# A fused attention and gated feed-forward kernel on one core: the side work of the last token pair placed by hand

## The chip, the core and the metric

The kernel runs on one core of a Trainium2 chip. A core has a matrix engine (TensorE, PE in the profile, with its weight loads as PEld), a vector engine (VectorE, DVE), a scalar engine (ScalarE, ACT), GpSimd (POOL), and a sync engine (SP) that here does little but issue DMA transfers, in the order of its own queue. Every engine runs its instructions in order and waits for others by semaphores. The metric is the device time of one execution in microseconds (us). Times below are medians of several runs; the profile is of one execution.

## The reference

x has two sequences of 2048 tokens with 2048 features, in float32. The output is x plus an attention and a feed-forward part, both of the normalised x:

```python
xn = _layernorm(x)
qkv = xn @ Wqkv + bqkv            # 2048 -> 3 * 512
q, k, v = split(qkv)              # one head, d = 512
attn = softmax(q @ k.T / sqrt(512)) @ v @ Wo + bo

q2 = xn @ Wq_w.T                  # router, 16 wide
top_vals, top_idx = top_k(q2 @ keys.T, 16)       # 16 of 64 experts
gate = one_hot sum of softmax(top_vals)
z = (xn @ A_w.T).reshape(64, 8) * gate           # rank 8 for each expert
ffn = z @ B_w.T * 2.0

out = x + attn + ffn
```

## The kernel before, in words

*Arithmetic.* Every float32 operand of a large matmul is split into a high part (`split_hi`, a cast on ACT, line 121) and a remainder (`split_lo`, a subtraction on DVE, line 124); a `product` (line 129) is three matmuls. Matrices are multiplied by a scheme of seven products in place of eight (P1, P2, P6, P5, P3, P7, P4), so operands and results are sums and differences of quarters.

*Stages.* Tokens go in 8 blocks of 512, two blocks make a pair. First all projections (q, k, the feed-forward z, v) are made: the first pair by itself, then pairs 1 to 3 in `phase`, seven phases for each pair. A phase has seven items: six feature pieces of 24 groups of matmuls with 512 columns, 5.45 us each at full pace, then V, the values and the router, in two pieces of 48 matmuls with 264 columns, 5.8 us each; some 44 us in all. For each piece `fetch` (line 605) issues the load of the weight `pw` on SP and splits it; `pw` has three slots to load into. After each item its results are evacuated (`phase_out`) and put down for a store; the stores are issued at the end of the next item (`flush`, line 162): q to `q_d`, k to `k_d`, values to `v_d`, z to `oz_d`. Then come the scores: `score(g)` (matmuls on line 1081), 56 for each pair of query blocks, each of six matmuls of 512 columns, 1.36 us, in step with the softmax and with the weighting of the values of the pair before. The output stage (line 1355) comes last, from 2029.7 us on.

*Side work.* `beside(j, ph)` gives each phase a list of small steps, and `phase` cuts the list into seven parts, one after each item. They are issued behind that item's instructions in the program; a scheduler then merges them with what is around. For pairs 1 and 2 the side work prepares the next pair's x. The last pair has no next pair, and prepares the scores:
- `key_list(a, b)`: keys 0 to 7 out of 16. A key (256 of the 512 features of a block of 512 tokens) loads two tiles `kr` from `k_d`, and has seven steps, one for each product. A step has at most one sum (lines 851 to 857), a cast and a subtraction into a tile `kst` of 512 words (line 124 and 121), and the store of the step before it to `kp_d` (line 843). The ring of `kst` has four slots, shared with the tiles `ev` and `zt` of the phases' results; in P4 it is a ring of three other slots.
- `query_steps(j, ring)`, pair 0's in P3 and P7, pair 1's in P4: twice, for d = 0 and 1, four loads of `qs` from `q_d` (line 892), four sums (lines 895 to 898), four stores to `qs_d` (line 902). The ring of four slots for pair 1 is `mid(0, 1, 2, 3)`, whose first two are also the slots of the value tiles `vs`.
- `query_load` and `query_split`: seven operands `qt` for a pair, one for each product (load on line 915), from `q_d` or `qs_d`. In P4 of the last pair `query_ready(0, n)` loads operand n + 1 and splits operand n.

The split operands `t` of the next phase are side work too (`split_steps`), and so are the sums in front of them. `mixed` interleaves several lists evenly.

*The first scores.* The operands `kt` of the scores are loaded back from `kp_d` (`key_load(i)`, line 937, two steps in a tile). Four of them are issued before the loop over g, the next after every second score. Side work of the score stages is put down for a g by `deal`: keys 8 to 11 beside the scores of the first pair (g from 0 to 55), keys 12 to 14 beside the second's, key 15 beside the third's, `query_steps` of pairs 2 and 3 and the preparation of the output weights (`combos`) later. NG1 is 56.

SP takes all loads and stores named here in one queue. A DMA on it waits for the landing of the one eight places before it, besides what its own data need.

The lines that matter for the order of P4's side work:

```python
ks["st"] = Ring(sb, "H6", "B18", "B19")
return [], [lambda: query_load(0, 0)] + mixed(
    [lambda n=n: query_ready(0, n) for n in range(7)],
    key_list(7, 8, False) + query_steps(1, mid(0, 1, 2, 3)),
)
```

Of the kernel before, what the change touches and what calls it, by code (L numbers as in the profile page):

```python
# [9 lines left out]
FR = mybir.dt.float32r  # L10
# [6 lines left out]
P = 128  # L17
# [45 lines left out]
def attn_ffn_kernel(ctx: ExitStack, tc, x, xT, wq, wv, wob, bqk, bv, bo, keysT, out):  # L63
# [17 lines left out]
    def big(*js):  # L81
        return Ring(sb, *(f"B{j}" for j in js))
# [569 lines left out]
    def mixed(*lists):  # L652

        n = max(map(len, lists))
        return [
            st for k in range(n) for ls in lists
            for st in ls[k * len(ls) // n : (k + 1) * len(ls) // n]
        ]

    def beside(j, ph):  # L660

        b00, b01, b10, b11 = (0, 0), (0, 1), (1, 0), (1, 1)
        more = j + 1 in PAIRS
        s0, s1 = stat_steps.get(2 * j + 2), stat_steps.get(2 * j + 3)
        if ph == "P1":
            t3 = sum_steps(j, nc.vector, b01, b11, b01, ALU.subtract)
            n10, n01, n11 = x_steps(j, *b10), x_steps(j, *b01), x_steps(j, *b11)
            if j > PAIRS[0]:
                return [], mixed(split_steps(j, "P2", *b10), n01[1], n11[1], t3)
            return (  # L670
                [n10[0], n01[0], n11[0]],
                mixed(n10[1], split_steps(j, "P2", *b10)) + mixed(n01[1], n11[1]),
            )
        if ph == "P2":
            t3 = sum_steps(j, nc.vector, b01, b11, b01, ALU.subtract) if j == PAIRS[0] else []
            return [], mixed(
                t3, sum_steps(j, nc.vector, b00, b01, b00, ALU.add), split_steps(j, "P6", *b00)
            )
        if ph == "P6":
            return [], mixed(  # L680
                sum_steps(j, nc.vector, b10, b10, b00, ALU.subtract),
                sum_steps(j, nc.vector, b00, b11, b00, ALU.subtract), split_steps(j, "P5", *b00),
                s0[:-2] if more else key_list(0, 3),
            )
        if ph == "P5":
            if more:
                steps = mixed(split_steps(j, "P3", *b11), s1[:-2])
                return [], s0[-2:-1] + steps[:6] + s0[-1:] + steps[6:]
            return [], mixed(split_steps(j, "P3", *b11), key_list(3, 5))
        if ph == "P3":  # L690
            if more:
                n = x_steps(j + 1, *b00)
                steps = mixed(split_steps(j, "P7", *b01), n[1][:2])
                return n[0], s1[-2:-1] + steps[:3] + s1[-1:] + steps[3:]
            return [], mixed(
                split_steps(j, "P7", *b01), query_steps(0, big(*GROUPS[3]), (0,))
            )
        if ph == "P7":
            if more:
                n = x_steps(j + 1, *b10)  # L700
                return n[0], mixed(split_steps(j, "P4", *b10), n[1][:2])
            return [], mixed(
                split_steps(j, "P4", *b10), query_steps(0, big(*GROUPS[3]), (1,)), key_list(5, 7)
            )
        if more:
            return x_steps(j + 1, *b01)[0] + x_steps(j + 1, *b11)[0], mixed(
                x_steps(j + 1, *b00)[1][2:], split_steps(j + 1, "P1", *b00)[:2],
            ) + mixed(split_steps(j + 1, "P1", *b00)[2:], x_steps(j + 1, *b10)[1][2:])
        ks["st"] = Ring(sb, "H6", "B18", "B19")
        return [], [lambda: query_load(0, 0)] + mixed(  # L710
            [lambda n=n: query_ready(0, n) for n in range(7)],
            key_list(7, 8, False) + query_steps(1, mid(0, 1, 2, 3)),
        )

    XU, YU, XV, YV = {}, {}, {}, {}

# [49 lines left out]
    def phase(j, ph, n):  # L766

        loads, steps = beside(j, ph)
        if not loads or callable(loads[0]):
            loads = [loads]  # L770
        ops = [tsp[j, ph, cp] for cp in range(NCP)]
        qr, gx = None, {}
        i = 2 * j + (ph in ("P3", "P7"))
        for m, it in enumerate(ITEMS[ph]):
            with behind("sp"):
                for st in loads.pop(0) if loads else []:
                    st()
            ps = [acc() for t in range(NT)] if it == "V" else acc()
            for g in range(2 if it == "V" else 1):
                w = ready.pop(n)  # L780
                n += 1
                if it != "V":
                    for c in range(HC):
                        product(
                            ps, lambda a: w[a][:, c * P : (c + 1) * P],
                            lambda b: ops[c // 2][b][:, c % 2, :], c == 0, c == HC - 1,
                        )
                else:
                    for cc in range(HC // 2):
                        c = g * HC // 2 + cc  # L790
                        for t in range(NT):
                            sl = slice(t * P, (t + 1) * P)
                            product(
                                ps[t][:, :VH], lambda a: ops[c // 2][a][:, c % 2, sl],
                                lambda b: w[b][:, cc, :], c == 0, c == HC - 1,
                            )
                fetch(n + 1)
            flush()
            if it == "V" and ph in ("P2", "P3"):
                qr = router_in()  # L800
            if it == NFP - 2:
                if qr is not None:
                    with behind("pe"):
                        gfs[i] = gates(i, wk)
                h = ph in ("P7", "P4")
                gx = {2 * h + k: gate(gfs[i], 2 * h + k) for k in range(2)} if ph in ("P2", "P3", "P7", "P4") else {}
            phase_out(j, ph, it, ps, qr, gx)
            if qr is not None and it in (0, 1):
                with behind("pe"):
                    if it == 0:  # L810
                        qT = router(qr)
                    else:
                        wk = choose(qT)
            for st in steps[m * len(steps) // 7 : (m + 1) * len(steps) // 7]:
                with behind("sp", "pe", "dve"):
                    st()
        return n
# [4 lines left out]
    ORDER = ("P1", "P6", "P2", "P5", "P3", "P7", "P4")  # L822
    NPAIR = NB // 2
    NKS = NK // 2
    ks = {"R": Ring(sb, "B25", "B26", "H7", "H8"), "st": big(27, 28, 29, 9)}
    qop, kop = {}, {}

    def key_steps(kb, d):


        v = {}
# [13 lines left out]
        def one(step):  # L845
            a00, a01, a10, a11 = (quad(a, h) for a in range(2) for h in range(2))
            tt = nc.vector.tensor_tensor
            out()
            src = {"P1": a00, "P2": a01, "P4": a11, "P5": a11, "P7": a10, "P6": a00, "P3": a01}[step]
            if step == "P5":  # L850
                tt(a11, a10, a11, ALU.add)
            if step == "P7":
                tt(a10, a00, a10, ALU.subtract)
            if step == "P6":
                tt(a00, a11, a00, ALU.subtract)
            if step == "P3":
                tt(a01, a01, a00, ALU.subtract)
            st = ks["st"]([P, 2, 2, P], FR, "kst")
            split_hi(st[:, :, 0, :], src)
            split_lo(st[:, :, 1, :], src, st[:, :, 0, :])  # L860
            v["out"] = kp_d[kb][ORDER.index(step)][:, :, :, d, :], raw(st)
# [56 lines left out]
    def query_split(j, n):  # L918
        hi, lo = qop[j, n]
        split_hi(hi, raw(lo))  # L920
        split_lo(lo, raw(lo), hi)

    def query_ready(j, n):
        if n + 1 < 7:
            query_load(j, n + 1)
        query_split(j, n)

    def key_load(i):

# [74 lines left out]
    n = 0  # L1004
# [23 lines left out]
    r_tp = mid(0, 1, 2, 3)  # L1028
    r_ph = wide(0, 1, 2)
    r_vt = wide(3, 4, 5, 9)  # L1030
    ks = {"R": mid(0, 1, 2, 3), "st": wide(0, 1, 2, 3, 4, 5)}
    S, tag_of, mbc, pt_, M, L, av, rl_, vt_, lsum = {}, {}, {}, {}, {}, {}, {}, {}, {}, {}
    ones = mid(2)([P, P], F32, "ones")
    nc.vector.memset(ones, 1.0)
# [376 lines left out]
    total = NPAIR * NG1  # L1411

    begin = [NG1 * (j + 1) + (9 if j in (0, NPAIR - 1) else 5) for j in range(NPAIR)]
    for i in range(4):
        key_load(i)
    side = {}

    def deal(g, steps, every=1):
# [11 lines left out]
        for k, st in enumerate(steps):  # L1430
            deal(g + (0, 3, 4)[k % 3] + 5 * (k // 3), [st])

    for n in range(4):
        keys(8 + n, 3 + 11 * n, 11 * n - 3 if n else 0)

    def small_ring():
        ks["R"], ks["st"] = mid(0, 1), mid(2, 3)

    deal(NG1 + 2, [small_ring])
    for n, g in ((12, NG1 + 6), (13, NG1 + 18), (14, NG1 + 49), (15, 2 * NG1 + 10)):  # L1440
        keys(n, g, g - 3)
    spaced(NG1 + 36, query_steps(2, r_tp))
    spaced(2 * NG1 + 19, query_steps(3, r_tp))
    slots = [2 * NG1 + k for k in (35, 40, 45)] + [3 * NG1 + k for k in (7, 12, 17, 22, 35)]
    for k, g in enumerate(slots):
        spaced(g, combos(k // ND, k % ND))

# [145 lines left out]
```

## Time and profile before

| | us |
|---|---|
| runs | 2637.84 median of 3 (2637.28 to 2642.51) |
| the profiled execution | 2639.59 |
| its span | 2637.8, at a granted TensorE clock of 0.994 |
| last pair's P6 ends, P5 starts | 1147.6 |
| last pair's P4, first scores | 1283.8 to 1335.4, 1335.4 to 1420 |
| second to fourth score stages, output stage | 1420 to 2029.7, from 2029.7 |

The profile names engines, lines and tiles: `PE L129 MATMUL acc<-t,pw` is a matmul of `product` that reads the tiles t and pw. In a timeline a row has its start, the time that it took, and how many such instructions ran in it one after the other; in brackets stands how long the engine was idle before it, and what released it. A list of waits adds these by line and releaser: total, times, longest. Rows on SP are issues of DMAs; the transfer lands some us later. In the part on DMA issues the last column is the median time from issue to landing.

### The profile page before, as it was taken

To read this page: it belongs to the slowest core of one execution; us is meant where nothing else is said; L and a number is where in the kernel's file an instruction comes from. 1 tells how busy PE (TensorE), PEld (TensorE's weight loads), DVE (VectorE), ACT (ScalarE), POOL (GpSimd) and SP (SyncE) were. 2 spreads that over 40 slices of the span, in tenths; PEclk is the share of its full clock that TensorE was granted. 3 is DMA by queue.
4 is the path that set the end of the run, shared out by engine and by line. 5 is a ranking of instruction groups with operands and counts; after the bars stand their busy time and mean duration, and the time that the engine had idled before them with its cause. 6 is when DMAs were issued, how large, how long until landed. Compare 5 with 4: busy or idle time off the path is not lost. (4 is left out here: it accounts for less than half of the span.)

```text
span 2637.8 us, 34791 instructions
## 1 busy us (share of the span) xinstructions
PE 2600.1 (99%) x12689; PEld 2194.4 (83%) x12689; DVE 1994.4 (76%) x2827; ACT 860.0 (33%) x1249; POOL 523.7 (20%) x315
## 2 busy tenths in 40 slices
PE   8999999999999999999989999999999999999999
PEld 7889888888888888888877887878777888888887
DVE  7557649867878677776769979979698776797675
ACT  4323323323332323343323434333254222332221
POOL 1311420001000010000000000000000666566664
PEclk9999999999999999999999999999999999999999
DMA  6667875668446673576999898889688554565542
GB/s 234 225 249 264 280 274 175 208 221 277 149 137 230 212 269 126 187 235 213 294 335 322 264 336 281 295 312 315 202 279 294 176 170 166 178 220 174 177 164 100
DMA packets 348043, 608.10 MB, mean 231 GB/s; under 512 B 28456, under 2 KB 151392, under 8 KB 347872
## 3 DMA queue, kind: packets, MB, share of 16 engines
q1 hardware_dynamic: 334912, 575.99, 65.1%
q10 hardware_dynamic: 12960, 29.89, 3.4%
q8 instruction: 100, 1.64, 0.3%
q14 instruction: 71, 0.58, 0.1%
HBM read 450.42 MB, written 155.35 MB: 230 GB/s over the span
## 5 line engine op out<-in xcount | busy, mean ns | idle before, releaser
L129 PE MATMUL acc<-t,pw 128*128 128x512 f32 x3024 | 697.4, 391 | 4.3 <-ACT t L121 1.8
L129 PEld LDWEIGHTS acc<-t,pw 128*128 128x128 f32 x3024 | 567.3, 188 | 123.8 <-ACT t L121 2.2
L1355 PE MATMUL acc<-wb,s 128*128 128x512 f32 x2688 | 609.8, 389 | 0.1
L1355 PEld LDWEIGHTS acc<-wb,s 128*128 128x128 f32 x2688 | 504.6, 188 | 105.1 <-ACT u L1367 0.6
L1339 POOL TENSOR_TENSOR xo<-xo,bo_bc 128x512 f32<-128x512 f32 x128 | 212.2, 1665 | 906.5 <-DMA bo_bc<-in_bo 612.8
L129 PE MATMUL acc<-ph,vt 128*128 128x512 f32 x1536 | 378.7, 391 | 4.4 <-issue 1.8
L1081 PE MATMUL acc<-qt,kt 128*128 128x512 f32 x1344 | 338.8, 394 | 9.1 <-DMA kt<-kp_d 5.5
L129 PEld LDWEIGHTS acc<-ph,vt 128*128 128x128 f32 x1536 | 288.7, 188 | 67.6 <-issue 3.2
L1081 PEld LDWEIGHTS acc<-qt,kt 128*128 128x128 f32 x1344 | 254.1, 190 | 67.3 <-DVE sp L1102 5.1
L121 ACT CAST pw<-pw 128x1024 fp32r<-128x1024 f32 (+1 forms) x168 | 177.7, 1059 | 343.2 <-PE acc L129 244.0
L124 DVE TENSOR_TENSOR pw<-pw 128x1024 fp32r<-128x1024 f32 (+1 forms) x168 | 213.0, 1268 | 78.6 <-ACT pw L121 77.9
L129 PE MATMUL acc<-xh,wh 128*128 128x512 f32 x1152 | 263.6, 390 | 0.0
L129 PEld LDWEIGHTS acc<-xh,wh 128*128 128x128 f32 x1152 | 215.6, 188 | 44.9
L129 PE MATMUL acc<-pw,t 128*128 128x264 f32 x2016 | 248.4, 285 | 4.6 <-ACT pw L121 3.7
L129 PEld LDWEIGHTS acc<-pw,t 128*128 128x128 f32 x2016 | 247.4, 189 | 6.3 <-ACT pw L121 3.9
L121 ACT CAST s<-xz 128x1024 fp32r<-128x1024 f32 x112 | 118.0, 1054 | 367.7 <-PE acc L1355 302.1
L124 DVE TENSOR_TENSOR s<-xz,s 128x1024 fp32r<-128x1024 f32 x112 | 172.8, 1545 | 39.4 <-ACT s L121 39.2
L124 DVE TENSOR_TENSOR wh<-wu,wh 128x512 fp32r<-128x512 f32 x96 | 84.1, 893 | 95.8 <-ACT wh L121 93.7
L518 POOL TENSOR_TENSOR zt<-zt,g 128x512 f32<-128x512 f32 x24 | 40.1, 1683 | 507.1 <-DMA g<-gd 241.4
L1344 DVE TENSOR_TENSOR xo<-xo,acc 128x512 f32<-128x512 f32 x128 | 86.9, 680 | 52.0 <-POOL xo L1385 25.3
L124 DVE TENSOR_TENSOR t<-xq,t 128x1024 fp32r<-128x1024 f32 x84 | 107.5, 1283 | 18.6 <-ACT t L121 18.1
L121 ACT CAST t<-xq 128x1024 fp32r<-128x1024 f32 x84 | 88.3, 1051 | 92.9 <-DVE xq L648 38.2
(165 smaller groups left out, 2508.3 us busy)
## 6 DMA issues: line engine op xcount, KB each, us to landing
vt<-v_d SPq DMA_DIRECT2D x128, 512.0 KB, 5.2
kt<-kp_d SPq DMA_DIRECT2D x224, 256.0 KB, 5.2
pw<-sq_d SPq DMA_DIRECT2D x72, 512.0 KB, 4.1
xo<-in_x SPq DMA_DIRECT2D x128, 256.0 KB, 3.1
xz<-oz_d SPq DMA_DIRECT2D x64, 512.0 KB, 4.6
out_y<-xo SPq DMA_DIRECT2D x128, 256.0 KB, 2.5
kp_d<-kst SPq DMA_DIRECT2D x112, 256.0 KB, 4.5
pw<-in_wq SPq DMA_DIRECT2D x54, 512.0 KB, 4.5
```

What stands on the lines that cost most here:

```text
L121: return nc.scalar.copy(hi, src)
L124: return (eng or nc.vector).tensor_tensor(lo, src, raw(hi), ALU.subtract)
L129: last["pe"] = nc.tensor.matmul(ps, st(a_), mv(b_), start=first and n == 0, stop=end and n == 2)
L518: nc.gpsimd.tensor_tensor(zt, zt, gx[n], ALU.mult)
L1081: last["pe"] = nc.tensor.matmul(ps, k[:, a, d, :], q[c][:, d, :], start=not more and d == 0 and i == 0, stop=d == 1 and i == 2, skip_group ...
L1339: nc.gpsimd.tensor_tensor(xs, xs, bo_bc[q // (NB // 2 * NH), c], ALU.add)
L1344: nc.vector.tensor_tensor(xs, xs, ps, op)
L1355: nc.tensor.matmul(ps, st[a_][:, kk, sl], mv[b_], start=not more and kk == 0 and n == 0, stop=kk == ND - 1 and n == 2, skip_group_check=more,)
```

## The change

1. `ks["n"]` is new: with 2, two steps of a key share one `kst` slot of 1024 words, the second step in the second half; seven steps take four slots in place of seven. With `small_ring` (from g = 58 on) it is 1, as before.
2. In P6, P5 and P7 of the last pair the last five, four and four key steps are no longer interleaved with the other side work, but come after it, at the end of the phase.
3. P4 of the last pair gets its side work by item, as a list of seven lists. `query_ready` goes; queries are loaded one step further ahead of their splits. The second group of query steps (load `l0`, `l1`, sums `s0`, `s1`, stores `o0`, `o1`) begins with the first item, where it stood at the end. The first four `key_load` move from in front of the loop over g into the last two items. The `kst` ring is `big(18, 19)`, two slots for two steps each.
4. Beside the first scores go three keys (8 to 10, at g = 5 + 14n, with their loads at 14n) in place of four. Key 11 takes the second stage's first place, the later keys are shifted by one place, and loads come two places ahead, not three.
5. `query_steps(3)` starts at 2NG1 + 35, not + 19, and the `combos` of the output weights are placed later: two in the third stage and six in the fourth, in place of three and five.

The number of instructions is the same on every engine.

```diff
         if ph == "P6":
-            return [], mixed(
+            steps = (
                 sum_steps(j, nc.vector, b10, b10, b00, ALU.subtract),
                 sum_steps(j, nc.vector, b00, b11, b00, ALU.subtract), split_steps(j, "P5", *b00),
-                s0[:-2] if more else key_list(0, 3),
             )
+            if more:
+                return [], mixed(*steps, s0[:-2])
+            ks_ = key_list(0, 3)
+            return [], mixed(*steps, ks_[:-5]) + ks_[-5:]
         if ph == "P5":
...
-            return [], mixed(split_steps(j, "P3", *b11), key_list(3, 5))
+            ks_ = key_list(3, 5)
+            return [], mixed(split_steps(j, "P3", *b11), ks_[:-4]) + ks_[-4:]
...
+            ks_ = key_list(5, 7)
             return [], mixed(
-                split_steps(j, "P4", *b10), query_steps(0, big(*GROUPS[3]), (1,)), key_list(5, 7)
-            )
+                split_steps(j, "P4", *b10), query_steps(0, big(*GROUPS[3]), (1,)), ks_[:-4]
+            ) + ks_[-4:]
...
-        ks["st"] = Ring(sb, "H6", "B18", "B19")
-        return [], [lambda: query_load(0, 0)] + mixed(
-            [lambda n=n: query_ready(0, n) for n in range(7)],
-            key_list(7, 8, False) + query_steps(1, mid(0, 1, 2, 3)),
-        )
+        ks["st"] = big(18, 19)
+        ql, qp = (lambda n: lambda: query_load(0, n)), (lambda n: lambda: query_split(0, n))
+        kl = lambda i: lambda: key_load(i)
+        k, (l0, s0, o0, l1, s1, o1) = key_list(7, 8, False), query_steps(1, mid(0, 1, 2, 3))
+        return [], [
+            [ql(0), ql(1), l0], [qp(0), ql(2), *k[:2]], [s0, qp(1), ql(3), *k[2:4]],
+            [o0, qp(2), ql(4), l1, k[4]], [qp(3), ql(5), *k[5:7]],
+            [qp(4), ql(6), s1, k[7], kl(0), kl(1)], [o1, kl(2), kl(3), qp(5), qp(6)],
+        ]
...
-            for st in steps[m * len(steps) // 7 : (m + 1) * len(steps) // 7]:
+            now = steps[m * len(steps) // 7 : (m + 1) * len(steps) // 7]
+            for st in now[0] if now and not callable(now[0]) else now:
                 with behind("sp", "pe", "dve"):
                     st()
...
-    ks = {"R": Ring(sb, "B25", "B26", "H7", "H8"), "st": big(27, 28, 29, 9)}
+    ks = {"R": Ring(sb, "B25", "B26", "H7", "H8"), "st": big(27, 28, 29, 9), "n": 2}
...
-            st = ks["st"]([P, 2, 2, P], FR, "kst")
+            n = steps.index(step)
+            if ks["n"] == 1 or n % 2 == 0:
+                v["st"] = ks["st"]([P, ks["n"], 2, 2, P], FR, "kst")
+            st = v["st"][:, n % ks["n"]]
...
-    for i in range(4):
-        key_load(i)
...
-    for n in range(4):
-        keys(8 + n, 3 + 11 * n, 11 * n - 3 if n else 0)
+    for n in range(3):
+        keys(8 + n, 5 + 14 * n, 14 * n)
 
     def small_ring():
-        ks["R"], ks["st"] = mid(0, 1), mid(2, 3)
+        ks.update(R=mid(0, 1), st=mid(2, 3), n=1)
 
     deal(NG1 + 2, [small_ring])
-    for n, g in ((12, NG1 + 6), (13, NG1 + 18), (14, NG1 + 49), (15, 2 * NG1 + 10)):
-        keys(n, g, g - 3)
+    for n, g in (
+        (11, NG1 + 6), (12, NG1 + 18), (13, NG1 + 48), (14, 2 * NG1 + 9), (15, 2 * NG1 + 19)
+    ):
+        keys(n, g, g - 2)
     spaced(NG1 + 36, query_steps(2, r_tp))
-    spaced(2 * NG1 + 19, query_steps(3, r_tp))
-    slots = [2 * NG1 + k for k in (35, 40, 45)] + [3 * NG1 + k for k in (7, 12, 17, 22, 35)]
+    spaced(2 * NG1 + 35, query_steps(3, r_tp))
+    slots = [2 * NG1 + 45, 2 * NG1 + 50] + [3 * NG1 + k for k in (7, 12, 17, 22, 38, 43)]
```

More of the change, by code (lines that the diff above doesn't have):

```diff
@@ L921, in query_split @@
         split_lo(lo, raw(lo), hi)
[L923 to L926, printed above, removed]
     def key_load(i):
@@ L1030, in attn_ffn_kernel @@
     r_vt = wide(3, 4, 5, 9)
-    ks = {"R": mid(0, 1, 2, 3), "st": wide(0, 1, 2, 3, 4, 5)}
+    ks = {"R": mid(0, 1, 2, 3), "st": wide(0, 1, 2, 3, 4, 5), "n": 2}
     S, tag_of, mbc, pt_, M, L, av, rl_, vt_, lsum = {}, {}, {}, {}, {}, {}, {}, {}, {}, {}
```

## The prediction

> **What bounds the kernel now.** I read the page's head first, then what TensorE (PE) waits for, then its timeline at each long wait, and last the timelines of ScalarE (ACT) and of the sync queue (SP), which are late there.
>
> ```profile
> span 2637.8 us, 34791 instructions
> ...
> PE 2600.1 (99%) x12689; PEld 2194.4 (83%) x12689; DVE 1994.4 (76%) x2827; ACT 860.0 (33%) x1249; POOL 523.7 (20%) x315
> ```
>
> PE is the bound, and the change leaves its instructions and all but a few places of their order as they are. So only PE's idle time, and the slow matmuls behind it, can move. Its waits from 1100 to 1440 us (total, times, longest):
>
> ```profile
> PE acc L1081 <- DMA kt<-kp_d: 5.5, 2, 4.7
> PE acc L1081 <- DVE qt L124: 2.2, 4, 0.7
> PE acc L129 <- ACT pw L121: 3.7, 1, 3.7
> PE acc L129 <- ACT t L121: 1.8, 1, 1.8
> ```
>
> Where they lie (start, length, then the wait before it):
>
> ```profile
> 1143.68 4.26 PE L129 MATMUL acc<-t,pw 128*128 128x512 f32 x18
> 1149.75 0.49 PE L129 MATMUL acc<-t,pw 128*128 128x512 f32 x1 [1.81 <-ACT t L121]
> 1151.50 10.86 PE L129 MATMUL acc<-t,pw 128*128 128x512 f32 x34 [1.26 <-DVE t L124]
> ...
> 1317.08 5.97 PE L129 MATMUL acc<-pw,t 128*128 128x264 f32 x48
> 1326.74 0.39 PE L129 MATMUL acc<-pw,t 128*128 128x264 f32 x1 [3.69 <-ACT pw L121]
> 1328.03 7.49 PE L129 MATMUL acc<-pw,t 128*128 128x264 f32 x47 [0.90 <-DVE pw L124]
> 1335.36 8.36 PE L1081 MATMUL acc<-qt,kt 128*128 128x512 f32 x36
> 1348.38 4.89 PE L1081 MATMUL acc<-qt,kt 128*128 128x512 f32 x13 [4.66 <-DMA kt<-kp_d]
> ```
>
> At full pace a 512-column matmul takes (4.26 − 0.39)/17 = 0.227 us, a 264-column one about 0.120. Measured against that:
> - A, the join of P6 and P5: 53 matmuls in 18.7 us instead of 12.0, less the 0.25 by which a row runs past its last start: **6.4 lost**. 3.1 of it is waiting; the rest is slow matmuls after the wait (13 of them 427 ns apart in the trace, 13 x 0.2 = 2.6).
> - C, the value pieces of P4: 96 matmuls from 1317.08 to 1335.36, 18.3 instead of 11.5: **6.8**. A further 0.6 is lost on the piece before (B).
> - D, the first scores: 4.85 late at 1348.38, then 13 matmuls in 4.6 instead of 2.95: **6.5**.
> - E and F: 1.0 at 1363 (the second kt wait) and, from 1418.65 to 1433.47, 34 matmuls and a small one in 14.8 instead of 7.9, **6.9**, at the join of the first two score stages (the qt waits).
>
> What is late at A and C:
>
> ```profile
> 1141.26 0.41 ACT L121 CAST kst<-kr 128x256 fp32r<-128x256 f32 x1 [4.26 <-DMA kp_d<-kst]
> ...
> 1307.92 0.46 SPq L605 DMA_DIRECT2D pw<-in_wv  x1
> ...
> 1313.29 0.52 SPq L843 DMA_DIRECT2D kp_d<-kst  x1
> ...
> 1318.87 0.43 SPq L605 DMA_DIRECT2D pw<-in_wv  x1
> ```
>
> At A a key step's cast has no free kst slot for 4.26 us, and the t casts of P5 stand behind it on ACT. At C the second value weight, due at 1322.8, is only issued at 1318.87, since SP stood from 1309 to 1313.29 before a key store. D is the same kind: the key tile of score 6 is issued at 1344.36, behind queries' and values' stores.
>
> **The change, part by part.** T = 1283.8 is the start of P4, S its end.
>
> *Two steps in a slot, key steps at the ends of phases.* Seven slots per key become four, and a cast waits for the store eight steps back, not four. In the changed order the second cast into a slot waits for no DMA, so the halves are tracked apart. The five last key steps of P6 now stand behind the P5 operands, and the first t casts come before the key casts that waited. With 6 key casts (0.41 each) ahead of the first t cast and no slot wait, the casts are done well before 1147.6. Bounds: 0, if slots are as late as now, to 6.4; I take **6.2**, since the wait was one slot's and has nothing else behind it. The key steps' own work (0.41 ACT, 0.34 to 0.42 DVE) is hidden under phases in which DVE is busy 35 of 44 to 51 us; uncovered, the five at the end would cost 5 x 0.8 = 4.
>
> *P4 by hand.* Here I expect the loss. In the changed order the first value weight's load moves from before to behind the whole chain of the second query group's work on SP: four query loads, four stores of sums, four more loads, a key store. Two of those loads go into the slots of P7's values, and so wait until value stores 2 and 3 have landed; those again wait for values 0 and 1 (two slots). The second four wait for the landing of the stores that they overwrite. With L for each landing: value store 0 at T + 5.1 (it was at 7.9, behind a 2.75 us wait of ACT for qt that goes); + L; 2.4 for evacuation and split of a value (4 small steps), 0.6 for the next: store 3 at 8.1 + L; + L + L for store and load; the sums (4 x 0.6, with a key split 0.35, a weight split 1.15 and a query split 1.2 between them, 5.1); + L; three issues 1.2; the load at 14.5 + 4L; + L; cast 1.05 and rest 1.25: the weight is ready at T + 16.9 + 5L. It is due at 6 x 5.45 = 32.7. The rows for L:
>
> ```profile
> v_d<-vs SPq DMA_DIRECT2D x32, 264.0 KB, 3.6
> ...
> qs<-q_d SPq DMA_DIRECT2D x32, 256.0 KB, 4.6
> qs_d<-qs SPq DMA_DIRECT2D x32, 256.0 KB, 5.4
> ```
>
> with 6.7 for P4's weights (1318.87 to the cast at 1325.61). 3.6 + 3.6 + 4.6 + 5.4 + 6.7 = 23.9, so PE waits 16.9 + 23.9 − 32.7 = 8.1, and 15 slow matmuls (220 instead of 120 ns at C) add 1.5. Behind the waiting cast on ACT stand the next query's and the second value weight's casts, which PE needs only after it; that second weight is issued 6 entries later and lands within the 5.8 us of the first piece. C and B (7.4) go, 9.6 comes: **−2.2**. Bounds: 3.5 for each landing gives 1.7 + 1.5 = 3.2, +4.2; 7.3 for each (the longest of P4's qt loads, 1320.17 to its cast at 1327.50) gives 20.7 + 2.6 (as at A), −15.9.
>
> This is where the skill would speak for the change. The trace's landings are 3.6 to 6.7 us. The Trainium skill ("DMA: Bandwidth & Descriptors", "Latency and other measured facts") puts memory latency at 0.2 us on average and 2 us at high load. An estimate by that page with 2 us gives no wait for this weight at all, and a sum 9.6 us better.
>
> *Key tiles 0 to 3 in P4.* They were issued before the scores too, but tiles for score 4 on came behind queries' stores. Now the first eight tiles stand before the value stores; the fifth is issued some 1.8 us after S (the last query store waits for a sum behind the first value's evacuation) and lands 3.3 to 4.8 us later, at S + 5.1 to 6.6, due at S + 4 x 1.36 = 5.45. At most 1.2 is left of 6.5: **+5.5** (5.3 to 6.5; 0 if SP is late throughout). The seven query loads (some 0.6 of SP each) are the same in number and only issued one step further ahead; they are priced at nothing, since what they could delay on SP, the weights, is in the chain above.
>
> *Three keys in the first scores.* One key less there: 11 small DVE operations of 0.34 (3.7 us) and 9 issues on SP of 0.57 (5.1 us), in a stretch whose DMA engines are busy all the time:
>
> ```profile
> 1335.40:1420.00 84.60, 79.11 (x341) 64.28 (x340) 69.62 (x133) 23.32 (x50) 0.00 (x0) 0.98 1.04 350
> 1420.00:1589.00 169.00, 165.43 (x713) 134.27 (x712) 150.64 (x244) 68.12 (x105) 0.00 (x0) 0.99 0.86 297
> ```
>
> (PE, PEld, DVE, ACT, POOL busy; clock; DMA share; GB/s.) E and F could give 0 to 7.9. At F the splits of j = 1's queries still alternate with the maxima on DVE; only the first comes ahead: **+1.5**. The key goes into the next stage, where DVE is busy 150.6 of 169, and query sums and one output-weight job (2.4 DVE) move on into later stages; wholly uncovered that is 3.7 + 2.4 = 6.1, wholly covered 0: **−1**. Each later stage has some 15 us of free DVE, but in pieces; if that cover fails at a join, the weights of the next value product are late next.
>
> Sum: 6.2 − 2.2 + 5.5 + 1.5 − 1 = **10 us gained**. The profiled execution took 2639.59 (span 2637.8 and 1.8 around it), 1.75 over the median of 2637.84; taken from the median: **2628**. 0.2%, what a measurement of this kernel can tell, is 5.3 us.
>
> At A the clock gate counts too. 1.81 and 1.26 us of waiting were followed by 13 matmuls at half pace. The Trainium skill ("TensorE: Matmul & The Clock Gate", "What's actually happening") has the slow clock follow an idle window of about 3.4 us; the row disagrees, so short waits carry a surcharge in my sum. By the rule, the first weight's wait of 8.1 would carry one as well, so it gives the same sum.
>
> **The rivals.**
> - *Better:* landings of 3.5, as the value stores' row has it, since query loads no longer block ACT. C 4.2, A 6.4, D 6, E and F 4, nothing lost later: 20.6, so **2617**. Against it: P4's DMA share was already 0.92.
> - *No change:* landings of 5.4 on the whole chain. Wait 27 − 15.8 = 11.2, with 2.6: C −6.4; A 6.2, D 4.5, moved work −4, E and F 0: **2637.5**. For it: the queries' rows of 4.6 and 5.4 and a kst median of 4.5 with 6.6 at the top.
> - *Slower:* the first value weight waits for the chain on SP at landings of 7.3: −15.9, D 5.5, and the kst slots free as late as now, so A 0; moved work −1. 11.4 lost: **2649**. It passes zero at L = 5.0 (5L − 15.8 + 2.6 − 7.4 = 5.5 − 1) and a loss of 5.3 at L = 6.1. For it: 6.7 and 7.3 in P4; against it: half the chain is value stores at 3.6.
> - *It doesn't do what it says:* the second step in a slot waits for the store of the first, A stays: 2634. The order speaks against it.
>
> **How the numbers follow.** Forecast 2628, own range 2622 to 2632: 0.46. Better 0.15, no change 0.21, slower 0.15, shared slot 0.03. Faster by over 0.2% is forecast and better, 0.61; within 0.2%, 0.24; slower 0.15. The range takes in most of better and no change: 2617 to 2641, leaving out some 0.08 below and 0.11 above.
>
> **What would show it.** No t wait at A. A pw wait at P4's first value piece, its load issued near T + 32 behind query loads that wait for value and query stores; no such wait, or one over 13 us, would break the forecast. No kt wait over 1.2 in the first scores. The waits at F a little shorter. PE's pace unchanged from 1440 on; new waits there for ph or vt would make the moved work dearer than −1.

## The result and the profile after

The changed kernel takes 2638.14 us (median of 20 runs, 2632.79 to 2647.17), the kernel before 2639.68 (20 runs, 2633.27 to 2645.58). The ratio is 0.9996, with a 95% interval of 0.9987 to 1.0005: no change that can be measured. The forecast was 2628, a gain of 10 us. The page's head of the changed kernel:

```profile
span 2634.8 us, 34738 instructions
...
PE 2596.4 (99%) x12689; PEld 2193.7 (83%) x12689; DVE 1987.5 (75%) x2827; ACT 859.2 (33%) x1249; POOL 521.7 (20%) x315
```

Its list of what PE waits for, from 1100 to 1440 us (total, times, longest):

```profile
PE acc L129 <- ACT pw L121: 9.9, 1, 9.9
PE acc L129 <- ACT ph L121: 3.0, 1, 3.0
PE acc L1089 <- DMA kt<-kp_d: 1.8, 1, 1.8
PE acc L1089 <- DVE qt L124: 1.6, 1, 1.6
```

The t waits are gone, the kt and qt waits have shrunk from 5.5 and 3.6 to 1.8 and 1.6. In their place stand a pw wait of 9.9, not 3.7, and a wait of 3.0 that was not there, for ph (the split softmax values that the value products take). Line numbers have moved: L1089 is the matmul of a score, L905 loads the query tiles qs, L915 stores their sums, L853 stores keys. The timeline of PE shows where they lie:

```profile
1145.50 14.69 PE L129 MATMUL acc<-t,pw 128*128 128x512 f32 x64
...
1322.13 14.61 PE L129 MATMUL acc<-pw,t 128*128 128x264 f32 x96 [9.86 <-ACT pw L121]
1336.58 11.06 PE L1089 MATMUL acc<-qt,kt 128*128 128x512 f32 x48
1349.44 70.69 PE L1089 MATMUL acc<-qt,kt 128*128 128x512 f32 x302 [1.81 <-DMA kt<-kp_d]
...
1435.12 0.50 PE L1142 MATMUL misc<-mq,onesr 48*128 48x512 f32 x1
1438.59 0.74 PE L129 MATMUL acc<-ph,vt 128*128 128x512 f32 x2 [2.97 <-ACT ph L121]
```

64 matmuls now run through the join of P6 and P5 without a break. P4's first value piece starts 10 us late, and its 96 matmuls take 14.6 us, not 11.5: half-pace matmuls follow the wait. The queue that brings its weight, SP, in the same profile:

```profile
1287.67 1.90 SPq L853 DMA_DIRECT2D kp_d<-kst  x3
1289.62 1.48 SPq L162 DMA_DIRECT2D v_d<-vs  x2
...
1294.80 1.18 SPq L162 DMA_DIRECT2D v_d<-vs  x2
...
1299.28 1.10 SPq L905 DMA_DIRECT2D qs<-q_d  x2
...
1306.93 2.06 SPq L915 DMA_DIRECT2D qs_d<-qs  x2
1309.08 5.09 SPq L905 DMA_DIRECT2D qs<-q_d  x4
1314.23 0.52 SPq L853 DMA_DIRECT2D kp_d<-kst  x1
1314.79 0.62 SPq L605 DMA_DIRECT2D pw<-in_wv  x1
```

This is the chain that the prediction added up. Each step waits for the one before: value stores 0 and 1 at 1289.62, 2 and 3 at 1294.80, the two query loads into their slots at 1299.28, the stores of sums until 1309, four more loads that take 5.09 us to issue because the stores must land first, and then the weight, 35.7 us after P4's start at 1279.1 (31.7 by the sum). The chain starts later than worked out: the first value store comes 10.5 us after P4's start, not 5.1. Its value is ready on DVE 7.8 us after the start, behind three sums of key steps among others, and then three key stores stand before it on SP. They are P7's un-mixed last key steps, so one part of the change delays another.

**Where the time went.** A single profile does not tell it, since executions of one kernel lie up to 20 us apart. The table adds up, for each profile, by how much the start of each matmul is later than 0.227 us (512 columns) or 0.120 us (264 columns) after the start of the one before. The stretches: 1100 to 1200 us; 60 us up to the first score; 70 us from it; from there to 30 us into the second score stage (join 1); to 20 us into the third (join 2); to 115 us into the fourth (join 3). The rest of the kernel loses 43 to 49 us in each profile, 25 to 28 of them in the first 100 us.

```
lost by PE, us               P6/P5    P4  first scores  join 1  join 2  join 3   all
before                         6.9    7.4      7.7        8.0     2.7    11.0    86.6
before, second profile         2.3    6.6      7.1        7.7     3.0     9.5    85.4
before, third profile          2.8    9.2     10.3        7.6     5.1    14.6    94.9
changed                        0.4   13.3      3.6       10.2     3.3     7.2    83.5
changed, second profile        0.4   12.4      3.6       10.0     9.4    10.2    91.4
```

Between the means of the rows (three of before, two of the changed kernel): +3.6 gained at P6/P5, −5.1 in P4, +4.8 in the first scores, −2.3 at join 1, −2.8 at join 2, +3.0 at join 3: 1.2 in all, and the medians differ by 1.5. P4, the first scores and join 1 repeat well enough to be read one by one; the kt wait in the first scores was 1.8 us with slow matmuls behind it in the first profile of the changed kernel and 3.4 us without them in the second, which lost 3.6 both times. Joins 2 and 3 vary from profile to profile by more than the kernels differ.

### The profile page after: what moved, and what is told of

Same layout as the page of the kernel before. It is cut to its first block, busy times and chain, and to the rows that moved or that the text cites. A ratio compares the mean times of both kernels' runs of the same rounds, so it can differ in the third digit from the quotient of the medians.

```text
span 2634.8 us, 34738 instructions
## 1 busy us (share of the span) xinstructions
PE 2596.4 (99%) x12689; PEld 2193.7 (83%) x12689; DVE 1987.5 (75%) x2827; ACT 859.2 (33%) x1249; POOL 521.7 (20%) x315
## 5 line engine op out<-in xcount | busy, mean ns | idle before, releaser
L1089 PE MATMUL acc<-qt,kt 128*128 128x512 f32 x1344 | 336.7, 393 | 3.5 <-DMA kt<-kp_d 1.8
L1089 PEld LDWEIGHTS acc<-qt,kt 128*128 128x128 f32 x1344 | 254.6, 190 | 59.2 <-DVE qt L124 2.7
L129 PE MATMUL acc<-pw,t 128*128 128x264 f32 x2016 | 249.3, 285 | 10.7 <-ACT pw L121 9.9
L129 PEld LDWEIGHTS acc<-pw,t 128*128 128x128 f32 x2016 | 247.8, 189 | 13.1 <-ACT pw L121 10.3
L121 ACT CAST ph<-sp 128x512 fp32r<-128x512 f32 x128 | 78.8, 617 | 141.7 <-PE acc L129 136.2
```

Source lines behind the costliest of these rows:

```text
L121: return nc.scalar.copy(hi, src)
L129: last["pe"] = nc.tensor.matmul(ps, st(a_), mv(b_), start=first and n == 0, stop=end and n == 2)
L1089: last["pe"] = nc.tensor.matmul(ps, k[:, a, d, :], q[c][:, d, :], start=not more and d == 0 and i == 0, stop=d == 1 and i == 2, skip_group ...
```

## The experiments

In each, theory 1 is that P4's value weight takes what the joins gained, theory 2 that the moved keys and late work (parts 4 and 5) lose it again in the score stages.

**The two kernels again**, unchanged.

> The changed kernel once more, for a second profile of it. If a loss is in the order of the work, it comes again: about 10 us of waiting before P4's first value piece, no t wait at the join of P6 and P5 (both theories). Theory 1 (what P4's join gains is lost on the value weight): the stretch from 1400 us on is as in the kernel before, within 2 us, and what differs there from profile to profile (the 3.0 us wait at 1435 us, the 1.8 us wait at 1854 us of the kernel before) is chance. Theory 2 (the moved keys cost it in the later stages): the 3.0 us wait at 1435 us and the 2.4 us wait at 1757 us come again. Time within 0.2% of the kernel before.

> The kernel before once more, for a second profile of it. The t wait at 1149 us (3 us), the pw wait at 1326 us (3.7) and the kt wait at 1348 us (4.7) come again if they are in the order of the work. The excess of PE between 1850 and 1900 us (5.9 us in the first profile) comes again if the later place of query sums and output-weight jobs is what took it away in the changed kernel, and not if it is chance.

> The kernel before, for a third profile: what its loss at the join of P6 and P5 is in a usual execution (6.9 and 2.3 us in two profiles). Near 2, and this term of the forecast was taken from an unusual profile; near 7, and the second was unusual.

The changed kernel again: 2639.45 (12 runs), ratio 0.9996 (0.9984 to 1.0007). The pw wait came again (9.2), and so did the ph wait at 1435 (3.0 to the hundredth) and the wait at 1757 for mq (the maxima that PE spreads), this time 4.2, not 2.4. So theory 1 is right on P4, and wrong that all after 1400 us is chance. The kernel before (2638.43 and 2647.96 us, one execution each) had its pw and kt waits again (3.5 and 4.6 in one, 4.8 and 6.4 in the other), and the loss from 1850 to 1900 us in one of the two (4.2 and 1.1). Its t waits were shorter:

```profile
1147.16 4.90 PE L129 MATMUL acc<-t,pw 128*128 128x512 f32 x19
1153.31 8.91 PE L129 MATMUL acc<-t,pw 128*128 128x512 f32 x38 [1.24 <-DVE t L124]
```

```profile
1148.85 0.50 PE L129 MATMUL acc<-t,pw 128*128 128x512 f32 x1 [0.87 <-ACT t L121]
1150.26 12.10 PE L129 MATMUL acc<-t,pw 128*128 128x512 f32 x52 [0.91 <-DVE t L124]
```

One wait of 1.24, and two of 0.87 and 0.91, against 1.81 and 1.26 followed by 13 slow matmuls in the profile that the forecast was made from: 2.3 and 2.8 us lost, not 6.9. About half of the 6.9 was the clock: from 1143.7 to 1194.4 us the granted clock was 0.93 in that profile, with 6.8 us at half clock from 1150.7, and 1.00 in the other two.

**Parts 1 and 2 alone**: P4, its ring and the score stages as before.

```diff
-        ks["st"] = big(18, 19)
+        ks.update(st=Ring(sb, "H6", "B18", "B19"), n=1)
...
+            [lambda n=n: query_ready(0, n) for n in range(7)],
+            key_list(7, 8, False) + query_steps(1, mid(0, 1, 2, 3)),
```

> Only parts 1 and 2 of the change (two steps in a slot, last key steps at the phases' ends); P4, its ring and the score stages are those of the kernel before. If the join of P6 and P5 gains by these parts alone, the t wait at 1149 us is gone and the waits at 1326 (pw) and 1348 (kt) are as before: 6 us below the kernel before. If the gain there needs the rest of the change, or is given back in P5, P7 or P4, the time is the kernel before's within 2 us.

> Parts 1 and 2 alone once more, for a second profile: 0.4 us lost at the join of P6 and P5 if these parts take that wait away every time; the total of PE's losses nearer to 83 than to the 76.9 of the first profile, since the median of its timed runs was 2641, if that profile was a lucky one.

2641.21 (12 runs; the second profile is of one execution of 2636.56), ratio 1.0004 (0.9992 to 1.0017): the 6 us didn't come. The join lost 0.4 in both profiles, so the wait is gone each time; P4, the first scores and join 1 lost what they lose in the kernel before (7.0 and 8.8, 8.9 and 8.1, 7.5 and 8.0). The first profile was one of the shortest executions (76.9 lost in all), the second lost 83.5. What parts 1 and 2 give is the 1.9 to 2.4 us of the second and third profile of the kernel before; that is at the edge of the interval (2.1 us), so the times neither show it nor rule it out.

**The value weights first**: the changed kernel with the query group's sums two items later, and its stores and second loads behind the second value weight.

```diff
-            ... [s0, qp(1), ql(3), *k[2:4]],
-            [o0, qp(2), ql(4), l1, k[4]], [qp(3), ql(5), *k[5:7]],
-            [qp(4), ql(6), s1, k[7], kl(0), kl(1)], [o1, kl(2), kl(3), qp(5), qp(6)],
+            ... [qp(1), ql(3), *k[2:4]],
+            [qp(2), ql(4), k[4]], [s0, qp(3), ql(5), *k[5:7]],
+            [o0, l1, qp(4), ql(6), k[7], kl(0), kl(1)], [s1, o1, kl(2), kl(3), qp(5), qp(6)],
```

> The changed kernel, with the sums of the second query group in the item of the fifth P4 piece, and its stores and second loads behind the loads of both value weights. Theory 1 (the weight's load stands behind that chain on SP): the first value weight is issued some 8 us earlier in P4 (26 to 28 us after its start, not 35.4) and PE waits 2 to 4 us before the value pieces in place of 9.9; the first kt waits grow by 0 to 5, since queries' stores now stand nearer to them; time 3 to 8 us below the changed kernel. Rival (the weight is late because its slot or the transfer engines are not free): the wait stays at 8 us or more, and the time is the changed kernel's.

2635.36 (12 runs), ratio to the kernel before 0.9978 (0.9967 to 0.9990), 4.1 us below the changed kernel timed beside it. PE in its timeline:

```profile
1313.71 0.39 PE L129 MATMUL acc<-pw,t 128*128 128x264 f32 x1 [1.45 <-ACT pw L121]
1315.00 13.65 PE L129 MATMUL acc<-pw,t 128*128 128x264 f32 x95 [0.91 <-DVE pw L124]
1331.57 5.87 PE L1089 MATMUL acc<-qt,kt 128*128 128x512 f32 x24 [2.92 <-DMA kt<-kp_d]
```

The weight was issued 27.3 us after P4's start, not 35.7, and the wait fell from 9.9 to 1.45 and 0.91. Its place on SP was the cause. But the first key tile is now 2.92 late: it stands behind the chain instead. With this wait and slow matmuls behind the first two (95 in 13.65 us, 11.7 at full pace) the stretch of P4 still loses 9.7.

**Value weights and eight key tiles first**: the whole query group behind both, and keys 8 to 10 four scores later.

```diff
-            [ql(0), ql(1), l0], ...
+            [ql(0), ql(1)], [qp(0), ql(2), *k[:2]], [qp(1), ql(3), *k[2:4]],
+            [qp(2), ql(4), k[4]], [qp(3), ql(5), *k[5:7]],
+            [l0, qp(4), ql(6), k[7], kl(0), kl(1)], [kl(2), kl(3), s0, o0, l1, s1, o1, qp(5), qp(6)],
...
-        keys(8 + n, 5 + 14 * n, 14 * n)
+        keys(8 + n, 9 + 14 * n, 4 + 14 * n)
```

> The changed kernel with the second query group's work behind both value weights and the first eight key tiles on SP, and the keys of the first score stage four scores later. By theory 1 PE waits under 1 us before P4's value pieces (9.2 to 9.9 in the changed kernel) and under 1 us for kt in the first ten scores; the stretch from the last feature piece of P4 to 1400 us loses 3 us or less in place of 16 to 17, and the time is 8 to 14 us below the changed kernel, about 2627, if nothing is lost again at the join of the first two score stages. If the queue only hands the wait on (the sums and key loads that come later now block DVE in the first scores), the same stretch loses 8 us or more and the time is that of the changed kernel with the value weights first, about 2635.

2636.82 (12 runs), ratio 0.9985 (0.9973 to 0.9997): the second case. PE, then SP:

```profile
1312.25 11.78 PE L129 MATMUL acc<-pw,t 128*128 128x264 f32 x96
1324.41 3.01 PE L1089 MATMUL acc<-qt,kt 128*128 128x512 f32 x12 [0.38 <-DMA kt<-kp_d]
...
1344.99 5.46 PE L1089 MATMUL acc<-qt,kt 128*128 128x512 f32 x12 [7.52 <-DMA kt<-kp_d]
```

```profile
1301.87 0.62 SPq L605 DMA_DIRECT2D pw<-in_wv  x1
...
1332.52 2.19 SPq L905 DMA_DIRECT2D qs<-q_d  x4
...
1338.35 2.97 SPq L915 DMA_DIRECT2D qs_d<-qs  x4
1341.41 0.52 SPq L162 DMA_DIRECT2D v_d<-vs  x1
1341.98 2.05 SPq L945 DMA_DIRECT2D kt<-kp_d  x4
```

P4 loses 0.8 in place of 13, with its value matmuls at full pace (96 in 11.78), and the first scores lose 12.5 in place of 3.6. The tile of score 8 stands behind query stores that wait for sums, which wait for loads that were issued only at 1332.52. The wait was handed to what stands next in the queue.

**The second half of the query group beside the scores**: as in the run before, with its load, sums and stores dealt to g = 2, 6 and 8, and keys 8 to 10 from g = 15 on.

```diff
+        late.extend([l1, s1, o1])
...
-            ... [kl(2), kl(3), s0, o0, l1, s1, o1, qp(5), qp(6)],
+            ... [kl(2), kl(3), s0, o0, qp(5), qp(6)],
...
+    deal(2, [late[0]])
+    deal(6, late[1:], 2)
-        keys(8 + n, 9 + 14 * n, 4 + 14 * n)
+        keys(8 + n, 15 + 13 * n, 11 + 13 * n)
```

> The changed kernel with the value weights and the first eight key tiles ahead on SP, as in the run before, and the second half of the query group (load, sums, stores) put beside scores 2 to 8, with the keys of that stage from score 15 on. If what was handed on there (7.7 us before score 8, its key tile behind query stores that waited for sums) is a matter of order in the queue alone, it goes: 3 us or less lost in P4 and 3 us or less in the first scores up to 1400 us, against 12.4 to 13.3 and 3.6 in the changed kernel. Losses at the later joins as in the changed kernel (10 at the first, 2 to 8 at the second, 5 to 8 at the third). Time about 2628 to 2632. If DVE or the transfers cannot take that work beside the first scores, 6 us or more is lost there or at the first join in addition, and the time stays at 2635 or more.

2632.52 (12 runs, 2626.41 to 2635.8), ratio 0.9961 (0.9947 to 0.9975). This version is faster than the kernel before, and by these ratios than the changed kernel (0.9996), which was not timed beside it. P4 loses 0.1, the first scores 7.6: the kt wait is 3.1, not 7.5, with slow matmuls behind it (120 in 29.1 us, 27.5 at full pace), and 2.1 are waits for ACT's copies of scores (sp). So the 3 us that were expected there were not met. Join 1 loses 10.7, as in the changed kernel.

**The score stages as before**: the changed kernel with parts 4 and 5 taken back.

```diff
-    for n in range(3):
-        keys(8 + n, 5 + 14 * n, 14 * n)
+    for n in range(4):
+        keys(8 + n, 3 + 11 * n, 11 * n - 3 if n else 0)
...
+    for n, g in ((12, NG1 + 6), (13, NG1 + 18), (14, NG1 + 49), (15, 2 * NG1 + 10)):
+        keys(n, g, g - 3)
...
-    spaced(2 * NG1 + 35, query_steps(3, r_tp))
+    spaced(2 * NG1 + 19, query_steps(3, r_tp))
+    slots = [2 * NG1 + k for k in (35, 40, 45)] + [3 * NG1 + k for k in (7, 12, 17, 22, 35)]
```

> The changed kernel with the places of keys 8 to 15, of the last query sums and of the output-weight jobs in the score stages as they were before (parts 4 and 5 undone). Theory 2 (these parts moved losses from one place to others): the 3.0 us ph wait at the join of the first two score stages (1435 us) and the mq wait of 2.4 to 4.2 us at 1757 us go, and the excess at 1850 us (4 to 6 us in the kernel before, 0.4 in the changed) comes back, so that the time is within 3 us of the changed kernel. Theory 1 (the value weight alone took the gain): the losses from 1400 us on stay as in the changed kernel, or vary by chance. Both expect the 9 to 10 us wait in P4 to stay.

2640.35 (12 runs), ratio 0.9997 (0.9982 to 1.0013). P4 still loses 13.9. Join 1 loses 7.5, as before the change, and the ph wait is gone. PE there:

```profile
1436.34 0.50 PE L1142 MATMUL misc<-mq,onesr 48*128 48x512 f32 x1
1436.77 2.08 PE L1089 MATMUL acc<-qt,kt 128*128 128x512 f32 x8
1438.69 1.52 PE L129 MATMUL acc<-ph,vt 128*128 128x512 f32 x6
```

Here, as in the kernel before, eight score matmuls stand between the second spread of the maxima (`misc`, made from `mq`) and the first value product; in the changed kernel the product stands right behind the spread. In both it starts at about 1438.6; in the one PE has worked until then, in the other it has waited 2.97 us. The operand has moved too. On DVE the subtraction that ph is made from stands ahead of the second mq in the kernel before, and behind it in the changed one:

```profile
1434.54 1.23 DVE L1150 TENSOR_TENSOR sp<-sp,mbc 128x1024 f32<-128x1024 f32 x1
...
1437.82 0.68 DVE L1124 TENSOR_TENSOR mq<-mhl,pick 48x512 fp32r<-48x512 f32 x1
```

```profile
1434.39 0.68 DVE L1132 TENSOR_TENSOR mq<-mhl,pick 48x512 fp32r<-48x512 f32 x1
...
1435.59 1.21 DVE L1158 TENSOR_TENSOR sp<-sp,mbc 128x1024 f32<-128x1024 f32 x1
```

So the first cast of ph on ACT comes 9.3 us after the first spread in the changed kernel (1437.92 and 1428.62) and 5.7 in the kernel before (1437.23 and 1431.55). An estimate from these rows: with the old order on DVE there would have been no wait, with the old order on PE alone about 1.2 us (2.97 less eight matmuls of 0.227). At about 1850 us 2.5 came back of the 4 to 6 that were expected, and the mq wait at 1757 was 2.0. The time is that of the changed kernel (0.9997 against 0.9996 of the kernel before): what parts 4 and 5 cost in one place they gave back in others.

**The last two output-weight jobs at an earlier place.**

```diff
-    ... [3 * NG1 + k for k in (7, 12, 17, 22, 38, 43)]
+    ... [3 * NG1 + k for k in (7, 12, 17, 22, 35, 40)]
```

> The changed kernel, with the last two output-weight jobs at g = 35 and 40 of the fourth score stage, not 38 and 43. If the excess of 4 to 6 us at 1850 us in the kernel before came from its job at g = 35 falling on the long reciprocal on DVE, it comes back here (2 us or more of waits between 1840 and 1860 us). If it came from the rest of what was moved, there is none, as in both profiles of the changed kernel.

One execution of 2642.76; at most 0.4 us lost between 1850 and 1900, no wait. The place of that job was not what the kernel before lost there.

**Late queries with the old stages**: the fastest version (2632.52), with four keys beside the first scores and the rest of parts 4 and 5 taken back as above.

```diff
-    for n in range(3):
-        keys(8 + n, 15 + 13 * n, 11 + 13 * n)
+    for n in range(4):
+        keys(8 + n, 15 + 10 * n, 11 + 10 * n)
```

> The same, with four keys beside the first scores (from score 15, ten apart) and the later keys, query sums and output-weight jobs where they were before the change. If parts 4 and 5 cost at the joins, the first join loses 7.5 to 8 us in place of 10, the second 2 to 3 in every profile, and about 1850 us 3 to 6 come back: time 0 to 4 us below the run beside it. If they are neutral, the two are within 2 us.

2637.53 (12 runs), ratio 0.9987 (0.9972 to 1.0003), 5 us above the run beside it. Join 1 lost 14.2, not 8: PE waited 5.7 for qt and 1.7 for a key tile, and the fourth key's steps ran to g = 51, into the query splits of the join. So it doesn't price parts 4 and 5, as it was meant to. That the fourth key no longer fits beside those scores when the query group is there is the likely reason; no run tested it by itself.

## Why the prediction was wrong

Of the 10 us that were forecast the table finds 1.2. Three terms failed: *three keys in the first scores* (+1.5 forecast, −2.3 measured), where a change of order made a new wait; *P4 by hand* (−2.2, −5.1), which was mis-sized; and the join of P6 and P5 (+6.2, +3.6), whose price came from an unusual profile.

- *Two steps in a slot, key steps at the ends (+6.2).* The mechanism held, the size failed. The wait went in every profile, so the rival in which the second step waits for the store of the first is out. But the loss was 2.3 and 2.8 us in two profiles out of three of the kernel before; the 6.4 that the forecast measured was the odd one. Parts 1 and 2 alone could not be told from no change.
- *P4 by hand (−2.2).* The mechanism was right: the first value weight waits behind the query chain on SP (9.9 and 9.2 waited, 8.1 forecast). Moving it ahead removed the wait. The term was mis-sized, −5.1: the slow matmuls behind it cost 2.9 (14.45 from 1322.13 to 1336.58, not 11.5), not 1.5, and the chain starts 5 us later than worked out, behind P7's key steps; the landings on it (value stores 3.5, the weight 6.2) were a little shorter than the rows used. The estimate with 2 us for each landing, by which there would have been no wait, fell.
- *Key tiles in P4 (+5.5).* Held: the first scores lose 3.6 in place of 7.1 to 10.3, 4.8 between the means. One kt wait of 1.8 and 3.4 us stayed, where at most 1.2 was expected. The second kt wait (E, 1.0) is in it, which the forecast counted with the next point.
- *Three keys in the first scores (+1.5 at E and F).* This step failed in its sign. The qt waits at join 1 did shrink, from 3.6 to 1.6, as forecast; but 3.0 of ph waiting came, and the join lost 2.3 more. The forecast looked at the waits that were there, and passed over a few moved places in the order of PE and DVE. Two of them made the new wait: the value product eight matmuls earlier on PE, and the subtraction in front of its operand behind the maxima on DVE. With parts 4 and 5 taken back the wait was gone and the join lost 7.5; which of the moved keys changed the order is open.
- *Moved work (−1).* −2.8 at join 2 and +3.0 at join 3, +0.2 in sum, but both within the spread of profiles of one kernel. All thirteen profiles tell more. From 1840 to 1900 us the seven with the old score stages lost 1.1 to 5.9, the six with the new ones at most 0.5: parts 4 and 5 took that loss away, and the job at g = 35 was not the reason; what was is open. Against it, the mq wait at about 1757 was 2.1 to 4.8 with the new stages and 0.3 to 3.3 with the old, and join 2 lost 9.4 to 9.7 in three of the six and at most 5.2 in the seven. So the moved work did cost at joins, as the forecast allowed, and gave about as much back elsewhere.
- *The outcome* was the rival "no change" with 2637.5, by part of its mechanism: the chain's price (−6.4 there, −5.1 measured). The rest of the agreement is luck: it had A at 6.2 (3.6), E and F at 0 (−2.3) and the moved work at −4 (+0.2), and these errors cancel. Its landings of 5.4 on the whole chain did not come, nor the slower rival's of 7.3; the longest on the chain was the weight's, 6.2.
- *The clock gate.* The granted clock in the traces is 1.0 or 0.5, and between 1100 and 2000 us its stretches at 0.5 last 3.4 us or a multiple of that. All 21 waits of PE of 3.49 us or more in the thirteen profiles came with such a stretch, and some of the shorter ones did. In the first profile of the changed kernel 3.4 us at half clock followed single waits of 1.81 and 1.62 us (1349.44 and 1421.76); in its second profile 3.44 and 1.63 us at the same places had none behind them, nor had 2.92 us in the run with the value weights first (24 matmuls in 5.87, 5.7 at full pace). The rule of the Trainium skill ("TensorE: Matmul & The Clock Gate", "What's actually happening"), an idle window of about 3.4 us, fits the long waits and the length of the stretches, but not the short waits that were enough; the row that the forecast set against it does not stand alone. What decides on a short wait, no run here shows.

## What to carry to other kernels

Before a loss of a few us is put into a sum, look at it in two or three profiles: one and the same join lost 2.3, 2.8 and 6.9 us, about half of the last at half clock, while the ph wait that the order decides came again to the hundredth. In an in-order DMA queue, a load with a due time belongs ahead of any chain of loads, sums and stores that wait for each other's landings; moving the chain back hands the wait to the next load behind it, until the chain stands where nothing behind it is due. After a reordering, compare the order on the bounding engine and on the engine that feeds it too: a product that moved up eight places, with its operand's preparation moved back, waited 3.0 us, more than the 2.0 of qt waits that the change removed there.

## What the runs showed of the hardware that was not expected

Executions of one and the same kernel lay between 2629.95 us (granted clock 0.997) and 2650.41 us (0.992) in a single session of 23 runs, and on the whole the longer runs were those with the lower clock (correlation −0.77). The profiles of that kernel show that they differ at the joins (2.3 to 6.9, 9.5 to 14.6) and in the first 100 us (25.2 to 28.3 lost), and in how many waits are followed by half clock. Whether one is varies at the same place, as the changed kernel's two profiles show. A wait that the order of instructions decides did not vary: the ph wait of the changed kernel was 2.97 us in both of its profiles and 2.97 and 2.98 in two of its variants; in the two that move the query group into the first scores it was 2.45 and 1.50.
